# Loads of x that don't wait for the averages' matrix, and layer 1 of an outlook network with three engines in program order and its transfers a column behind their source

## The chip, the cores and the metric

One core of one Trainium2 chip runs the kernel. The metric is the device time of one execution in microseconds (us), taken as the median of several runs; a profiled execution has a span of its own, a little longer. TensorE does the matrix work (PE in the views; PEld is its weight load), VectorE (DVE) and ScalarE (ACT) the elementwise work, GpSimd (POOL) some of it, SyncE (SP) only asks for transfers. SyncE and ScalarE each ask for transfers on a queue of their own, q1 and q10 in the profile.

## What is computed

The input x is 8 images of 56 x 56 positions with 384 channels, in float32. Two layers follow one another, each x + layer(group norm of x). A layer computes values v and attention logits from every position by a projection, takes a softmax over the 9 positions of a 3 x 3 window, and weighs the values with it:

```python
def _gn(v, G=32, eps=1e-5):
    g = v.reshape(B_, H_, W_, G, C_ // G)
    m = jnp.mean(g, axis=(1, 2, 4), keepdims=True)
    s = jnp.var(g, axis=(1, 2, 4), keepdims=True)
    return ((g - m) / jnp.sqrt(s + eps)).reshape(v.shape)
...
# layer 0: 12 heads; each position has 9 x 9 weights and adds to 9 places
attn = jax.nn.softmax(a * d ** (-0.5), axis=-1)
out = jnp.einsum('bnhpq,bnqhd->bnphd', attn, v_unf).reshape(b, h, w, k2, c)
...
# layer 1: 6 heads; each position has 9 weights and gathers from 9 places
a = jax.nn.softmax(a.reshape(B, H * W, heads, k * k), axis=-1)
y = jnp.einsum('bpKhd,bphK->bphd', patches, a)
return y.reshape(B, H, W, C) @ W_proj + b_proj
...
x = x + _L0_conv_ref(_gn(x), L0_conv_Wv, L0_conv_Wa, L0_conv_Wo)
x = x + _L1_conv_ref(_gn(x), L1_conv_W_attn, L1_conv_b_attn, L1_conv_W_v, L1_conv_b_v, L1_conv_W_proj, L1_conv_b_proj)
```

## The kernel before

Two images make a pair, so there are four pairs; a column of a pair is 112 rows of one x coordinate, and there are 56 columns. Seven columns make a group (the code's `px`), eight groups a pair, 32 groups a layer.

*Start.* Pair 0 of x is loaded in 14 blocks of 4 columns (L132 in the profile, on SyncE), transposed on TensorE (L122), copied out by ScalarE into 14 "homes" all over the on-chip memory, and its statistics are taken by VectorE. Four buffers hold loaded blocks: two in `xr`, two in `vp_first`. The group averages need a matrix `gmat`, made by three matmuls from a 0/1 matrix `gsel` that GpSimd writes. `gsel` is in a pool of its own that is closed again, and the `patch` pool, opened later, lies on the same memory. `keep_block` then stores the transposed blocks to `xT` in the DRAM, in the order 2, 3, ... 13, 0, 1, since later steps read them again: `xin` has two buffers, which are the homes of blocks 0 and 1, and block 2 is loaded into the first of them. These stores are in SyncE's program order, with zero fills of the tables between them.

*Layer 0.* One step per column: three projections for logits, softmax, weights, spread into a table `ztab0` in the DRAM. Once per group, `z` (the weights, read back as bands) and `vp` (the values, read back as patches) are loaded and contracted into `yT`, which is projected and added to x. The result is stored as `x1` for layer 1.

*Layer 1.* A step of the loop is one column m of a group g. `attend` projects 128 tokens to logits and values (`bank`, from `wc_t`); VectorE adds the biases into `lgt` and `v`, and `spread` stores v to `vtab1` (ScalarE's queue). When the group's columns are through, the following go on beside the columns of the next group:

- `regroup`: logits stored to `lgtab` (ScalarE's queue), read back as `at` (SyncE's queue), both at m = 0;
- `weigh` at m = 2: maximum, subtraction (VectorE), exponential (ScalarE), sum, reciprocal (VectorE), multiplication (GpSimd);
- `move` at m = 3: three matmuls `pw`, nine small copies into `wz` (ScalarE), one store to a table `ztab1` (ScalarE's queue);
- `fetch` in the same step: `vp` loaded from `vtab1`, `z` loaded from `ztab1` (SyncE's queue), and 14 jobs put on a list: four contractions (`pc`, copied to `yT` by ScalarE), four turns, six projections (`po`, added to `x1t` by VectorE), the last three with a turn each. A turn transposes a column of the result and copies it to `ot`; after the fourth and the seventh a store to `out` follows.

The jobs fall due four columns after `fetch`; two of them run in every step, one before `attend` and one after it:

```python
jobs.run(base + step, 1)
...
jobs.run(None, 1)
fetch(g - 1, base + step + 4)
```

`load(g + 1)` of the layer's input `x1t` is asked for at m = 4, into one of four buffers; `normed` on ScalarE normalises it at m = 6 and m = 0. `z` has four buffers in the memory of layer 0's two `z` tiles.

*Order.* Only TensorE's instructions are kept in the order in which the program names them (`tc.keep_in_program_order`); a scheduler orders the other engines by its own estimates, but for the instructions of SyncE that go through the `InOrder` wrapper in layer 0. Each engine then carries out its list in order, and waits at an instruction until what it needs is there.

Of the kernel before, what the change touches and what calls it, by code (L numbers as in the profile page):

```python
# [15 lines left out]
def two_outlook_layers(  # L16
# [35 lines left out]
    P = 128  # L52
# [85 lines left out]

    shift = const.tile([R, K, R], F32, name="shift")
    nc.gpsimd.memset(shift, 0.0)  # L140
    for k in range(-1, 2):
        s = shift[:, k + 1, :]
        nc.gpsimd.affine_select(
            out=s, in_=s, compare_op=ALU.not_equal, fill=1.0,
            base=k, pattern=[[-1, R]], channel_multiplier=1,
        )
    for b in range(1, IMG):
        nc.gpsimd.memset(shift[:, 2, b * H : b * H + 1], 0.0)
        nc.gpsimd.memset(shift[:, 0, b * H - 1 : b * H], 0.0)


    PH_ALL = K * HEADS0
    inside = const.tile([R, K, PH_ALL], F32, name="inside")
    nc.gpsimd.memset(inside, 1.0)
    for b in range(IMG):
        for pi, row in ((0, b * H), (2, b * H + H - 1)):
            nc.gpsimd.affine_select(
                out=inside[:, pi, :], in_=inside[:, pi, :], compare_op=ALU.not_equal, fill=0.0,
                base=-row, pattern=[[0, PH_ALL]], channel_multiplier=1,
            )  # L160
# [3 lines left out]
    with tc.tile_pool(name="setup", bufs=1) as setup, tc.tile_pool(  # L164
        name="ps_setup", bufs=2, space=PS
    ) as ps_setup:
        gsel = setup.tile([G, C], F32, name="gsel")
        nc.gpsimd.memset(gsel, 1.0)
        nc.gpsimd.affine_select(
            out=gsel, in_=gsel, compare_op=ALU.is_ge, fill=0.0,  # L170
            base=0, pattern=[[1, C]], channel_multiplier=-GC,
        )
        nc.gpsimd.affine_select(
            out=gsel, in_=gsel, compare_op=ALU.is_ge, fill=0.0,
            base=GC - 1, pattern=[[-1, C]], channel_multiplier=GC,
        )
        for i in range(NCH):
            pg = ps_setup.tile([P, C], F32, tag="pg", name=f"pg_{i}")
            matmul(pg, gsel[:, i * P : (i + 1) * P], gsel, start=True, stop=True)
            nc.vector.tensor_scalar_mul(gmat[:, i, :], pg, 1.0 / GC)  # L180

    NZERO = (EP0 - E0) * ROW0
    zeros = const.tile([R, NZERO], F32, name="zeros")
    nc.gpsimd.memset(zeros, 0.0)
# [51 lines left out]
    nc.gpsimd.memset(eps_t, EPS)  # L236
# [119 lines left out]
    patch = ctx.enter_context(tc.tile_pool(name="patch", bufs=2))  # L356
# [11 lines left out]
    def projected(name):  # L368
        return patch.tile([P, NCH, PX, IMG, H], F32, tag="yT", name=f"yT_{name}", bufs=1)

    def rows_to_patches(vp, table, px, r0, py, npy, sx):
        first = (px * (R + GAP) + GAP - MARGIN + r0) * sx * C
        nc.sync.dma_start(
            vp,
            bass.AP(
                table.tensor, table.offset + first, [[C, vp.shape[0]], [py * sx * C, npy], [1, C]]
            ),
        )
# [13 lines left out]
    def layer0(late, pools):  # L392
# [49 lines left out]
        def blocks_in(flat, n, at=0):  # L442
# [19 lines left out]
            *blocks_in(projected("first").rearrange("p i m b y -> p (i m b y)"), 1),  # L462
# [6 lines left out]

        def first_load(blk):  # L470
            xr = more[:R, blk // 2 % 2] if blk % 2 else xr_tile(0, blk)
            stats_load(0, blk, sync, xr)

        sync = InOrder(nc.sync)
        NXR = 4
# [26 lines left out]
        for i in range(NCH):  # L502
            for pi in range(K):
                natural = wn[:, i, pi * NP0 : (pi + 1) * NP0].rearrange("c (j q h) -> c q j h", j=K, q=K2)
                nc.gpsimd.tensor_tensor(
                    wa_t[:, i, pi * NL : (pi + 1) * NL].rearrange("c (q j h) -> c q j h", q=K2 - 1, j=K),
                    natural[:, : K2 - 1],
                    natural[:, K2 - 1 :].to_broadcast([P, K2 - 1, K, HEADS0]),
                    ALU.subtract,
                )  # L510
# [113 lines left out]
        def fetch_v(pair, px):  # L624

            vps[:] = [patch_tiles(f"0_{pair}_{px}", b) for b in range(IMG)]
            for b in range(IMG):
                rows_to_patches(vps[b], vtab0, px, b * H, PY0, NPY0, SX0)
# [80 lines left out]
        def upkeep(step):  # L709

            pair, c = divmod(step, W)
            if pair == 0:

                for n in (2 * step, 2 * step + 1):
                    if n < NBLK:
                        keep_block(0, (n + 2) % NBLK)
                if c == 3:
                    sync.dma_start(wo_t, wo0.rearrange("(i p) n -> p i n", p=P))
                if c == 8:
                    for z in zs:  # L720
                        nc.gpsimd.memset(z, 0.0)
# [56 lines left out]
    def layer1(pools, base, last_of_layer0, late_w):  # L778
        io = pools.enter_context(tc.tile_pool(name="io1", bufs=2))
# [4 lines left out]

        def load(g):
            pair, px = divmod(g, NPX)

            if g % 4 == 3:
                t = late_w.tile([P, NCH, T], F32, tag="xres", name=f"x1t_{g}")
            else:  # L790
                t = io.tile([P, NCH, T], F32, tag="x1t", name=f"x1t_{g}", bufs=3)
            nc.sync.dma_start(t, x1s[pair][px])
            x1ts[g] = t.rearrange("p i (m r) -> p i m r", m=PX)

        def normed(g, m0, m1):
# [4 lines left out]
            for lo, hi in ((first + m0, min(cut, first + m1)), (cut, first + m1)):  # L800
# [3 lines left out]
                for i in range(NCH):  # L804
                    for b in range(IMG):
                        rows = slice(b * H, (b + 1) * H)
                        nc.scalar.activation(  # L807
                            to[:, i, :, rows], x1ts[g][:, i, lo - first : hi - first, rows],
                            AF.Identity,
                            bias=bias[:, i, b : b + 1], scale=scale[:, i, b : b + 1],  # L810
                        )
# [5 lines left out]
        nc.sync.dma_start(wc_t[:, :, :NA1], wa1.rearrange("(i p) n -> p i n", p=P))  # L817
        nc.sync.dma_start(wc_t[:, :, NA1:], wv1.rearrange("(i p) n -> p i n", p=P))
# [8 lines left out]

        NZ = 4
        half_z = NPY1 * PY1 * ROW1
        zs1 = [  # L830
            zs[n // 2].rearrange("p n e -> p (n e)")[: SX1 * SY1, n % 2 * half_z : (n % 2 + 1) * half_z]
            .rearrange("p (n e) -> p n e", n=NPY1)
            for n in range(NZ)
        ]

        def attend(g, m):

            col = g * PX + m
            if col % SB == 0:
                return  # L840
# [5 lines left out]
            nc.vector.tensor_add(staged[-1][1][:, len(staged[-1][0])], pa[:, :NA1], ba_t)  # L846
            staged[-1][0].append(col // SB * NT + tile_no)
            v = work.tile([P, C], F32, tag="v", name=f"v_1_{col}", bufs=5)
            nc.vector.tensor_add(v, pa[:, NA1:], bv_t)  # L849
            for lo, n_col, row, n in parts_of(tile_no):  # L850
                c = col - col % SB + n_col
                spread(nc.scalar, vtab1, SX1, c % W, 1, row, v[lo : lo + n])
# [6 lines left out]
        def regroup(g):  # L859
# [3 lines left out]
            nc.scalar.dma_start(  # L863
# [5 lines left out]
            )  # L869
            lgs[g] = work.tile([R, PX, K2, HEADS1], F32, tag="at", name=f"at_1_{g}")  # L870
            nc.sync.dma_start(
# [7 lines left out]

        def weigh(g):  # L880

            at = lgs[g]
            heads_last = [R, PX, K2, HEADS1]
            mx = work.tile([R, PX, HEADS1], F32, tag="mx", name=f"mx1_{g}")
            nc.vector.tensor_reduce(mx, at.rearrange("r x k h -> r x h k"), AX.X, ALU.max)
            nc.vector.tensor_tensor(at, at, mx.unsqueeze(2).to_broadcast(heads_last), ALU.subtract)
            nc.scalar.activation(at, at, AF.Exp)
            den = work.tile([R, PX, HEADS1], F32, tag="den", name=f"den1_{g}")
            nc.vector.tensor_reduce(den, at.rearrange("r x k h -> r x h k"), AX.X, ALU.add)
            nc.vector.reciprocal(den, den)  # L890
            nc.gpsimd.tensor_tensor(at, at, den.unsqueeze(2).to_broadcast(heads_last), ALU.mult)  # L891

        def move(g):
# [14 lines left out]
            for kj in range(K):  # L908
                dst = wz[:, kj * K * ROW1 : kj * K * ROW1 + PX * step].rearrange("r (m e) -> r m e", e=step)
                dst = dst[:, :, : K * ROW1].rearrange("r m (e h o) -> r e m h o", e=K, h=HEADS1)  # L910
                for e in range(K):
                    nc.scalar.copy(dst[:, e, :, :, 0], pw[:, e, :, kj, :])
            table = ztab1[g % NTAB]
            nc.scalar.dma_start(
# [7 lines left out]
        def fetch(g, due):  # L922
# [5 lines left out]
            for b in range(IMG):  # L928
                rows_to_patches(vps[b], vtab1, px, b * H + MARGIN - 1, PY1, NPY1, SX1)
            for b in range(IMG):  # L930
                z, vp = zs1[(g * IMG + b) % NZ], vps[b]
                bands(
                    nc.sync, z, ztab1[g % NTAB], LINE1, SLOT1, ROW1, MARGIN - 1, GROUPS1,
                    b, PY1, NPY1,
                )

                def contract(t, b=b, z=z, vp=vp):
# [12 lines left out]
                    nc.scalar.copy(  # L950
# [9 lines left out]
            def project_out(half, j):  # L960
# [5 lines left out]
                nc.vector.scalar_tensor_tensor(  # L966
# [3 lines left out]
            def turn(m):  # L970
# [8 lines left out]
                nc.scalar.copy(fetch.ot[:, m - lo, :], pt)  # L979
                if m == hi - 1:  # L980
                    nc.sync.dma_start(
# [17 lines left out]
        for step in range(NG * PX + 4):  # L999
            g, m = divmod(step, PX)  # L1000
            jobs.run(base + step, 1)
            if step == 0:
                last_of_layer0(base + step + 5)
            if step == 4:
                for wz in wzs:
                    nc.gpsimd.memset(wz, 0.0)
            if g < NG:
                attend(g, m)
            if g and m == 0:
                regroup(g - 1)  # L1010
                stage(g)
            if m == 4 and g + 1 < NG:
                load(g + 1)
# [4 lines left out]
            jobs.run(base + step, 1)  # L1018

            if g and m == 2:  # L1020
                weigh(g - 1)
            if g and m == 3:
                move(g - 1)
                while not clear_bands.done:
                    jobs.run(None, 1)
                fetch(g - 1, base + step + 4)
# [47 lines left out]
```

## Time and profile before

| what | value |
|---|---|
| median of 3 runs | 3564.13 us (3562.12 to 3565.1) |
| span of the profiled execution | 3582.0 us, mean granted clock of TensorE 0.982 |
| layer 0's columns begin / end | about 64.6 us / 2313 us |
| first and last store lgtab<-lgt | 2375.2 us / 3525.9 us |
| DMA | 839.34 MB, 234 GB/s on average |

Busy time is in us with its share of the span. In the slices each digit is a fortieth of the span, in tenths. A group's line gives engine, operation, tiles as out<-in, count, busy time, and the idle time of the engine before it with what ended it. What the transfers of layer 1 take from issue to landing (median, us):

```profile
vp<-vtab SPq DMA_DIRECT2D x64, 945.0 KB, 10.7
...
x1t<-x SPq DMA_DIRECT2D x32, 1176.0 KB, 10.9
...
z<-ztab SPq DMA_DIRECT2D x128, 258.4 KB, 5.5
```

And what SyncE itself waited for in layer 1, from 2420 us on (us in total, times, longest):

```profile
SPq L871 <- DMA lgtab<-lgt: 370.0, 30, 18.2
SPq L320 <- DMA ztab<-wz: 297.6, 31, 13.8
SPq L373 <- DMA vtab<-v: 144.0, 25, 9.8
SPq L981 <- ACT ot L979: 63.7, 22, 13.0
```

L871 is the read of `at`, L320 the read of `z`, L373 that of `vp`, L981 the store of `out`.

### The profile page before, as it was taken

What the parts mean: (1) busy time and instruction counts of PE and PEld (TensorE: products, weight loads), DVE (VectorE), ACT (ScalarE), POOL (GpSimd) and SP (SyncE); (2) the same over time, 40 slices, a digit from 0 to 9 for tenths busy, and PEclk for the clock granted to TensorE, in tenths of its full rate; (3) what the DMA queues carried; (4) which work ended last, traced back from release to release, by engine and by line L of the source; (5) the groups of instructions that cost most, each with busy time, mean ns of one, the idle gap of its engine ahead of it and who ended that gap; (6) DMA issues with size and microseconds to landing.
All of it is one profiled execution on the core that took longest, in us unless ns stands there. A gap on an engine that the chain in (4) does not pass through costs nothing. (4 is left out here: it accounts for less than half of the span.)

```text
span 3582.0 us, 72091 instructions
## 1 busy us (share of the span) xinstructions
PE 3460.1 (97%) x29014; PEld 2370.5 (66%) x29014; DVE 1918.4 (54%) x4648; ACT 1165.9 (33%) x2727; POOL 986.7 (28%) x1409
## 2 busy tenths in 40 slices
PE   7799999999999999999999999989999999999998
PEld 5577767777777777677767777655565665656555
DVE  5666666667766766677666666533222222222222
ACT  3233323332333233333223322232333433334332
POOL 3443444434443444334434444410000000000000
PEclk8899999999999999999999999999999999999999
DMA  7999988688877777887667676687778787778876
GB/s 238 274 299 278 270 274 272 211 252 265 282 237 238 247 248 248 258 275 249 213 194 246 214 223 228 223 266 192 208 198 225 192 215 207 201 210 212 217 215 160
DMA packets 691453, 839.34 MB, mean 234 GB/s; under 512 B 302191, under 2 KB 595375, under 8 KB 687023
## 3 DMA queue, kind: packets, MB, share of 16 engines
q1 hardware_dynamic: 329614, 576.00, 50.9%
q10 hardware_dynamic: 361504, 258.73, 26.9%
q8 instruction: 228, 3.74, 0.4%
q14 instruction: 107, 0.87, 0.1%
HBM read 512.95 MB, written 321.66 MB: 233 GB/s over the span
## 5 line engine op out<-in xcount | busy, mean ns | idle before, releaser
L119 PE MATMUL bank<-wa_t,xn 128*112 128x288 f32 x4032 | 1088.3, 409 | 19.7 <-ACT xn L529 16.5
L119 PEld LDWEIGHTS bank<-wa_t,xn 128*112 128x112 f32 x4032 | 693.9, 177 | 272.8 <-issue 33.4
L119 PE MATMUL po<-yT,wo_t 128*128 128x448 f32 (+1 forms) x2304 | 818.8, 495 | 5.3 <-DVE x1t L679 4.8
L568 POOL TENSOR_TENSOR at<-at,den 112x972 f32<-112x972 f32 x224 | 504.8, 2254 | 1157.9 <-DVE den L567 1105.1
L119 PEld LDWEIGHTS po<-yT,wo_t 128*128 128x128 f32 x2304 | 432.8, 191 | 293.7 <-issue 189.4
L119 PE MATMUL pc<-z,vp 121*32 121x49 f32 (+1 forms) x17664 | 494.4, 256 | 44.2 <-DMA z<-ztab 19.6
L119 PEld LDWEIGHTS pc<-z,vp 121*32 121x32 f32 (+1 forms) x17664 | 448.1, 132 | 121.1 <-issue 94.4
L119 PE MATMUL bank<-wc_t,xn 128*128 128x438 f32 x1176 | 496.7, 560 | 4.4 <-DMA wc_t<-in_wv 3.2
L544 DVE TENSOR_REDUCE mx<-bank 112x36 f32<-112x324 f32 x672 | 327.4, 487 | 323.1 <-PE bank L119 316.0
L119 PE MATMUL bank<-wv_t,xn 128*128 128x384 f32 x1176 | 419.2, 493 | 0.0
L891 POOL TENSOR_TENSOR at<-at,den 112x378 f32<-112x378 f32 x32 | 30.2, 944 | 1132.0 <-DVE den L890 853.9
L119 PEld LDWEIGHTS bank<-wc_t,xn 128*128 128x128 f32 x1176 | 220.3, 197 | 183.0 <-issue 172.2
L545 DVE TENSOR_TENSOR at<-bank,mx 112x324 f32<-112x324 f32 x672 | 328.5, 489 | 21.0 <-DVE den L567 0.3
L549 ACT ACTIVATE at<-at 112x972 f32<-112x972 f32 x224 | 227.0, 1014 | 343.6 <-DVE at L545 319.6
L807 ACT ACTIVATE xn<-x1t,bias,scale 128x168 f32<-128x168 f32 (+4 forms) x498 | 213.7, 503 | 324.7 <-DMA x1t<-x 236.9
L119 PEld LDWEIGHTS bank<-wv_t,xn 128*128 128x128 f32 x1176 | 219.9, 191 | 140.0 <-issue 19.3
L966 DVE SCALAR_TENSOR_TENSOR x1t<-po,bo_t,x1t 128x448 f32<-128x448 f32 (+1 forms) x192 | 120.1, 625 | 322.9 <-PE po L119 322.9
L846 DVE TENSOR_TENSOR lgt<-bank,ba_t 128x54 f32<-128x54 f32 x196 | 41.3, 211 | 440.0 <-PE bank L119 439.8
L591 POOL TENSOR_TENSOR pre<-at,at 112x108 f32<-112x108 f32 (+1 forms) x440 | 239.0, 543 | 125.3 <-DVE wt L614 110.7
L613 ACT COPY wt<-pw 112x120 f32<-112x120 f32 x224 | 58.0, 259 | 659.3 <-PE pw L119 607.5
L561 DVE TENSOR_TENSOR d<-at 112x432 f32<-112x432 f32 x224 | 141.3, 631 | 199.7 <-ACT at L549 199.7
L658 ACT COPY yT<-pc 128x294 f32<-128x294 f32 x256 | 103.4, 408 | 372.2 <-PE pc L119 327.0
(95 smaller groups left out, 2818.5 us busy)
## 6 DMA issues: line engine op xcount, KB each, us to landing
z<-ztab SPq DMA_DIRECT2D x64, 2352.0 KB, 15.6
vp<-vtab SPq DMA_DIRECT2D x64, 1536.0 KB, 7.4
ztab<-wt ACTq DMA_DIRECT2D x336, 183.8 KB, 6.3
vp<-vtab SPq DMA_DIRECT2D x64, 945.0 KB, 10.7
xres<-xT SPq DMA_DIRECT2D x32, 1176.0 KB, 11.2
x1t<-x SPq DMA_DIRECT2D x32, 1176.0 KB, 10.9
xin<-xT ACTq DMA_DIRECT2D x54, 672.0 KB, 4.9
z<-ztab SPq DMA_DIRECT2D x128, 258.4 KB, 5.5
```

The source lines that it names most:

```text
L119: tc.keep_in_program_order(nc.tensor.matmul(*args, **kwargs))
L544: nc.vector.tensor_reduce(mx[:, pi, :], pl.rearrange("r q a -> r a q"), AX.X, ALU.max)
L545: nc.vector.tensor_tensor(at[:, pi], pl, mx[:, pi, :].unsqueeze(1).to_broadcast([R, K2, PH]), ALU.subtract)
L549: nc.scalar.activation(at, at, AF.Exp, scale=SCALE0)
L561: nc.vector.tensor_add(d4, at[:, :, 0:4], at[:, :, 4:8])
L568: nc.gpsimd.tensor_tensor(at, at, den.unsqueeze(2).to_broadcast([R, K, K2, PH]), ALU.mult)
L591: nc.gpsimd.tensor_tensor(dst, terms[0], terms[1], ALU.add)
L613: nc.scalar.copy(mid[:, 0 : E0 : E0 - 1, :], pw[:, 0 : E0 : E0 - 1, :])
L658: nc.scalar.copy(yT[:, :, :, b, rows_of], pc.rearrange("p i n y m -> p i m (n y)"))
L807: nc.scalar.activation(to[:, i, :, rows], x1ts[g][:, i, lo - first : hi - first, rows], AF.Identity, bias=bias[:, i, b : b + 1], scale=sca ...
L846: nc.vector.tensor_add(staged[-1][1][:, len(staged[-1][0])], pa[:, :NA1], ba_t)
L966: nc.vector.scalar_tensor_tensor(res, po[:, :n], bo_t[:, j : j + 1], res, ALU.add, ALU.add)
```

## The change

At the start, `gsel` is put into the memory of `yT`, and GpSimd makes it first, in program order. The loads of x into `vp_first` have nothing to wait for any more. The blocks 0 and 1 are kept second, after 2 and 3. In layer 1, VectorE, ScalarE and SyncE are put in program order. Each transfer is asked for about a column after the work that makes its source, so that an engine that waits in its list waits little. `regroup` becomes `keep_logits` (m = 0) and `read_logits` (m = 1); `weigh` is split into `weigh` (m = 3, to the exponential) and `share` (m = 4); `move` is at m = 5 and `fetch` at m = 0 of the group after, with the jobs due three columns later. Within `fetch`, `z` is read before `vp`. `x1t` is loaded at m = 1 and has five buffers; the fifth is a half of a `z` tile, so `z` has three buffers left. The stores of `v` come behind the second job of their step, and the stores of `out` go to ScalarE's queue. The last group runs through these steps faster (`last`).

```diff
+    gpsimd = InOrder(nc.gpsimd)
+    patch = ctx.enter_context(tc.tile_pool(name="patch", bufs=2))
+    yT_first = projected("first")
+    yT_flat = yT_first.rearrange("p i m b y -> p (i m b y)")
...
-        gsel = setup.tile([G, C], F32, name="gsel")
-        nc.gpsimd.memset(gsel, 1.0)
+        gsel = yT_flat[:G, :C]
+        gpsimd.memset(gsel, 1.0)
...
-            xr = more[:R, blk // 2 % 2] if blk % 2 else xr_tile(0, blk)
+            xr = more[:R, blk % 2] if blk % NXR > 1 else xr_tile(0, blk)
...
-                        keep_block(0, (n + 2) % NBLK)
+                        keep_block(0, n ^ 2 if n < 4 else n)
...
     def layer1(pools, base, last_of_layer0, late_w):
+        vector, scalar, sync = (InOrder(e) for e in (nc.vector, nc.scalar, nc.sync))
...
-            if g % 4 == 3:
+            if g % 5 == 3:
                 t = late_w.tile([P, NCH, T], F32, tag="xres", name=f"x1t_{g}")
+            elif g % 5 == 4:
+                t = halves[3][:, : NCH * T].rearrange("p (i t) -> p i t", i=NCH)
...
             for b in range(IMG):
-                rows_to_patches(vps[b], vtab1, px, b * H + MARGIN - 1, PY1, NPY1, SX1)
+                bands(
+                    sync, zs1[(g * IMG + b) % NZ], ztab1[g % NTAB], LINE1, SLOT1, ROW1, MARGIN - 1,
+                    GROUPS1, b, PY1, NPY1,
+                )
+            for b in range(IMG):
+                rows_to_patches(sync, vps[b], vtab1, px, b * H + MARGIN - 1, PY1, NPY1, SX1)
...
-                    nc.sync.dma_start(
+                    scalar.dma_start(
                         of[pair * R : (pair + 1) * R, px * PX + lo : px * PX + hi, :],
...
-        for step in range(NG * PX + 4):
+        for step in range((NG + 1) * PX):
             g, m = divmod(step, PX)
+            done, last = g - 1, g == NG
+            read, first, second, moved = (0, 2, 3, 4) if last else (1, 3, 4, 5)
             jobs.run(base + step, 1)
...
+            if g and m == first:
+                weigh(done)
+            if g and m == second:
+                share(done)
+            if g and m == moved:
+                move(done)
+            store = lambda: None
             if g < NG:
-                attend(g, m)
+                store = attend(g, m)
+            jobs.run(base + step, 1)
             if g and m == 0:
-                regroup(g - 1)
+                keep_logits(done)
                 stage(g)
-            if m == 4 and g + 1 < NG:
-                load(g + 1)
+            store()
             if m == 6 and g + 1 < NG:
                 normed(g + 1, 0, 3)
             if m == 0 and 0 < g < NG:
                 normed(g, 3, PX)
-            jobs.run(base + step, 1)
-            if g and m == 2:
-                weigh(g - 1)
-            if g and m == 3:
-                move(g - 1)
+            if m == 1 and g + 1 < NG:
+                load(g + 1)
+            if g > 1 and m == 0:
                 while not clear_bands.done:
                     jobs.run(None, 1)
-                fetch(g - 1, base + step + 4)
+                fetch(done - 1, base + step + 3)
+            if g and m == read:
+                read_logits(done)
+            if last and m == 5:
+                fetch(done, base + step + 1)
```

## The prediction

> **What bounds the kernel now.** I read the page's shares and slices first, then TensorE's busy time by stage, then what TensorE waits for, then the chain that ended last.
>
> ```profile
> PE 3460.1 (97%) x29014; PEld 2370.5 (66%) x29014; DVE 1918.4 (54%) x4648; ACT 1165.9 (33%) x2727; POOL 986.7 (28%) x1409
> ...
> PE   7799999999999999999999999989999999999998
> ```
>
> TensorE is the bound. The change removes no matmul, so it can only win back time in which TensorE waits. The windows (columns: stretch, its length, PE busy and instructions, granted clock, DMA share, GB/s) say where that is:
>
> ```profile
> 0.00:20.00 20.00, 9.62 (x33) 1.00 0.65 188
> 20.00:50.00 30.00, 23.27 (x122) 0.84 1.02 287
> 50.00:100.00 50.00, 43.07 (x187) 0.89 0.66 231
> 100.00:200.00 100.00, 81.05 (x418) 0.90 0.94 292
> ...
> 500.00:1000.00 500.00, 499.60 (x4479) 1.00 0.80 252
> ...
> 2800.00:3000.00 200.00, 190.26 (x1356) 0.94 0.78 210
> 3000.00:3200.00 200.00, 191.02 (x1426) 0.97 0.78 204
> ```
>
> Three stages: the start (up to 200 us) has 43 us of idle TensorE; layer 0 after it has almost none; layer 1 (2313 us on) loses some 5% again, and there the granted clock dips too. One wait at the start and the waits of layer 1 (window 2420 to the end; us in total, times, longest):
>
> ```profile
> 120.16 0.55 PE L122 MATMUL pt<-ident,xr 112*128 112x112 f32 x4
> 134.98 5.35 PE L119 MATMUL bank<-wa_t,xn 128*112 128x288 f32 x12 [14.27 <-ACT xn L529]
> ```
> ```profile
> ACT xn L807 <- DMA x1t<-x: 236.9, 22, 12.7
> ...
> PE pc L119 <- DMA z<-ztab: 16.2, 10, 3.0
> PE pw L119 <- POOL at L891: 13.4, 11, 2.7
> ```
>
> The listed waits of TensorE in layer 1 are short: 48 us in all (the two above, 11.3 without a named cause, 5.6 on the copies out of pc, 1.6 on ot). Behind them stands the chain of one group:
>
> ```profile
> 2800.45 12.59 DMA ztab<-wz
> 2813.43 4.44 DMA z<-ztab
> 2818.01 2.12 PE pc L119 x48
> ```
> ```profile
> 2397.55 6.31 DMA ztab<-wz
> ```
>
> The weight table takes 12.6 us to land when SyncE's queue carries vp and x1t beside it. In the first group it is 6.3 us, and there, by the trace's packets, the first 2.5 stood beside the end of an x1t load; then its 1,008 packets passed in about 2 us. Then z is read, and the contraction waits for it.
>
> The pace: the 32 stores lgtab<-lgt are issued from 2375.2 to 3525.9 us, so a group takes 37.1 us. Its matmuls at full clock, by their start-to-start times: wc_t 2.2 us x 49 tiles in 8 groups = 13.5; pc 2 x (1.55 + 1.20) = 5.5; po 3 x 2.26 + 3 x 1.70 = 11.9; seven transposes 3.0; pw 0.7. Sum 34.6 us. So 31 groups hold 78 us of loss, waits and slow clock together.
>
> **What the Trainium skill says.** "TensorE: Matmul & The Clock Gate", Part 1 (The HAM clock gate): after an idle window TensorE's clock is halved until it has been busy for a while. The trace agrees: behind the 14.27 us wait twelve matmuls took 5.35 us against 3.08 elsewhere, and after the 2.05 us wait at 2818 the next six took 3.57 against 2.47. So a wait of 2 us costs up to 4. "DMA: Bandwidth & Descriptors", Queues, rings and completion order: SyncE and ScalarE own one queue each on the same 16 engines, each consumed in order, the engines alternating between the two. The trace agrees: an x1t load issued at 2840.75 had its first packet at 2845.5, behind the vp and out packets asked for before it. "PSUM — Partial Sum Buffer", Engine vs sequencer instructions: VectorE's and ScalarE's queues are strictly first in, first out, so an early wait blocks all behind it. The trace agrees: transposes into pt ended at 2809.7 and were copied at 2813.0, behind a normalisation that waited for x1t until 2811.75.
>
> **The change part by part.**
> *Start.* Before, the second to fourth load of x go out at 9.43 us, when the matmuls on gsel have read a buffer that vp_first lies on; after, gsel lies in yT, and four loads go out from 0.8 us. From 20 to 50 us the DMA share is 1.02: the 11.0 MB issued from 9.43 us end by some 51, which is about 268 GB/s. All 11.7 MB from 1.5 us at that rate end at 45: -6.5 us. The gsel steps move to the head of GpSimd's list (from 5.1 to about 3 us, the sum of the durations before it), which keeps TensorE ready for it.
> *Blocks 0 and 1 kept early.* The xin load of block 2 needs the buffer of block 0, whose store goes last (issued 110.8 to 125.5). That is the 14.27 us wait and 2.3 us of slow clock. With the order 2, 3, 0, 1 the store goes out before 60 us, and block 2 is due at about 102: the wait vanishes. DMA is at 0.94 there and gets less time for the same stores, and the two 4 us memsets of z now stand between GpSimd's multiplications; I give back 3 us. Start in all: -20 us (10 to 27).
> *x1t loads* three columns earlier, with a fifth buffer: ends the 236.9 us for which ScalarE stood at the normalisation. TensorE waited 1.2 us for that; by itself nothing.
> *Logits, weights, contraction.* weigh moves from m=2 to 3, share 4, move from 3 to 5, the contraction from four columns behind the move to five. Columns m=0..2 hold two po jobs and take 6.5 us, m=3..6 about 4.2. The logits and ztab get slack, and pw's 13.4 us and z's 16.2 us of waits lose their old cause.
> *Program order on SyncE.* The list is now, per group: 4 z, 2 vp, x1t, at. The z reads wait for ztab, and vp, x1t and at stand behind them, on one queue. The at read, which took 2.5 us to land with the queue to itself, now lands behind 4 MB. From it follow weigh, pw, ztab, and the next z: a loop that goes round once per group. Its length, from landing of at to landing of the next:
> - at to issue of ztab: mx, subtract, exp, den, reciprocal, the GpSimd multiply, pw and nine copies took 6.6 us in the last group (3533.1 to 3539.7). In program order exp holds up ScalarE, and about 2 us of the copies and DMA issues it held stand before the nine: 8.3 us.
> - ztab to the first z packet: SyncE's queue is empty then. 1.2 us to ztab's first packet, 2.0 for its packets, 1.3 until SyncE is released, 1.1 to z's first packet: 5.6. Bounds: this, and the 8.5 us that the last group's ztab took beside vp and an out store, 9.6 in all. I take the lower, as nothing of SyncE's is under way.
> - By the packets of the trace a group costs the 16 engines 5.3 us for z, 8.0 for vp, 2.9 for x1t, 0.8 for at: 17.0. ScalarE's queue puts about 4.1 between (lgtab 0.8, vtab of three columns 2.2, the rest of an out store). 21.1 at the 1.05 that the share reaches when both queues run: 20.1 us.
> - to VectorE's start: 0.6.
> Sum 34.6 us, the same as TensorE's own. So the loop and TensorE set the pace together, and a late landing in either is a wait of 1 or 2 us at the contraction or pw of m=5, since exp holds the copies that free pc. With 1 us of such waits and slow clock per group I take 35.6: 31 x (35.6 - 37.1) = -46 us.
> *Ends.* First logits behind an x1t load: +5 us. At the end z stands before vp and the contraction comes later, but six more po jobs and the whole of group 30 cover the last chain; before, 2.7 us of wait stood there. In all +4 us.
> *out stores* on ScalarE's queue instead of SyncE's (3.8 us of engines per group): hidden, counted above.
> Sum: -20 - 46 + 4 = -62: 3502 us; I say 3500.
>
> **Rivals.**
> *TensorE's pace alone*, as the change intends: at lands within some 23 us of m=0 and no wait is left. For it: z, vp and weigh have slack in columns. Against: the loop's sum leaves none. With 0.3 us of small waits per group: 31 x (34.9 - 37.1) = -68, start -20, ends +2: 3478 us.
> *The loop sets the pace clearly.* More of ScalarE's stores between, or a ztab of 6.5: 36.8 us. 31 x 0.3 = -9, start -20, ends +4: 3539 us. For it: DMA has no idle stretch between ztab and at, so all that is late adds.
> *The loop is much longer, and the time gets worse.* ztab at 8.5 as in the last group, since out stores and vtab stand before it in ScalarE's queue: 34.6 + 4.0 = 38.6 us. 31 x 1.5 = +47, ends +4, start -20: 3595 us. For it: the chain of before shows what sharing does to ztab (12.6). Against: SyncE's queue is empty while ztab is written.
> *The start gives nothing*, because DMA is at 0.94 to 1.02 there and the wait turns up later: 3522 us with the rest as forecast. Against it: the window 50 to 100 us has a share of 0.66.
>
> **How the numbers follow.** Both set the pace (35.2 to 36.2 us, 3488 to 3522; the start that gives nothing counted in): 0.45. TensorE's pace: 0.18. The loop clearly (to 37.5, 3560): 0.22. Much longer: 0.15. The first two are faster, of the third nine in ten, of the last none: faster by over 0.2% (below 3557) 0.82, within 0.2% (to 3571) 0.05, slower 0.13. Range 3465 to 3575: below lies a TensorE that never waits together with a start that gives its most, above the last case but its edge.
>
> **What would show it.** Right: at<-lgtab taking over 10 us to land instead of 2.5; VectorE's mx waiting for it in many groups; the lgtab stores 35 to 36 us apart; DMA still near 0.8 with idle stretches while at is worked on; the 14.27 us gone. Wrong: lgtab stores under 35 us apart and mx never waiting (then TensorE's pace), or 37 and more (then the longer loops); the 14 us turning up in another ScalarE wait before 200 us; SyncE issuing vp or x1t ahead of z.

## The result, and the profile after

The changed kernel takes 3614.69 us (3612.19 to 3625.53) against 3564.61 us: 1.014 times the time of before, 95% interval 1.012 to 1.0161. It is slower by 50 us; 62 us less had been forecast. The profiled execution of before lies 17 us above its median, so the two traces show only 3614.5 - 3582.0 = 32.5 us of the 50.

Shares and slices of the changed kernel's page:

```profile
PE 3459.2 (96%) x29014; PEld 2362.1 (65%) x29014; DVE 1918.4 (53%) x4648; ACT 1180.6 (33%) x2727; POOL 985.7 (27%) x1409
...
PE   7899999999999999999999999889999999999998
```

TensorE is busy for the same time as before (3460.1), with the same instructions: in these two traces all of the loss is idle TensorE, 155 us instead of 122. The windows, in the same stretches as before (stretch, length, PE busy and instructions, clock, DMA share, GB/s):

```profile
0.00:20.00 20.00, 11.54 (x55) 0.97 0.88 264
20.00:50.00 30.00, 17.85 (x122) 0.78 1.03 313
50.00:100.00 50.00, 44.82 (x175) 0.83 0.66 219
100.00:200.00 100.00, 85.73 (x532) 0.97 0.97 305
500.00:1000.00 500.00, 499.77 (x4476) 1.00 0.82 257
2800.00:3000.00 200.00, 191.14 (x1465) 0.98 0.77 207
3000.00:3200.00 200.00, 186.49 (x1445) 0.98 0.75 203
```

The start does slightly better, and layer 0 is as it was. The place of work tells more than busy time: the last four matmuls of pw in layer 0 come at 2313.3 us instead of 2324.5, so the start brought 11 us between these two traces (in the traces of the experiments with the same start they come at 2312.6 to 2323.2 us). The first store of lgtab comes only 4.5 us earlier (2370.7), the last one 18.3 us later (3544.2), and from there to the end it is 70.3 us instead of 56.1. A group takes 37.86 us instead of 37.12. TensorE's work in the tail, from the last store on, grew by 9.1 us, because a group is now finished later; its idle time there grew by 5. So the opening of layer 1 gives back 7 of the 11 us, and the groups lose most: the stretch between the first and the last store is 22.8 us longer, and TensorE is idle in it for 79.5 us instead of 51.3. TensorE's waits in layer 1 (waits of the changed kernel from 2420 to 3540 us; total, times, longest):

```profile
PE pc L119 <- ACT yT L132: 40.4, 24, 3.8
PE bank L119 <- ACT xn L132: 27.7, 22, 2.2
```

These two had been 5.6 and 0; z and pw, for which TensorE waited 29.6 us before, are gone from the list. ScalarE had become the engine that TensorE waits for. The timeline of ScalarE ahead of one such wait (start, length, instruction; ACTq is the issue of a transfer; in brackets the idle time before):

```profile
2695.46 0.52 ACT L132 ACTIVATE at<-at 112x378 f32<-112x378 f32 x1 [3.70 <-DVE at L132]
2695.88 0.46 ACT L132 COPY ot<-bank 112x384 f32<-112x384 f32 x1
2696.37 0.33 ACTq L132 DMA_DIRECT2D out<-ot  x1
2696.80 2.22 ACTq L132 DMA_DIRECT2D vtab<-v  x2
2699.06 0.44 ACT L132 COPY yT<-pc 128x336 f32<-128x336 f32 x1 [2.72 <-DVE v L132]
```

The contraction that TensorE runs next needs the last copy, at 2699.06. Ahead of it in ScalarE's list stand exp, late because at had landed late (VectorE's mx, the maximum that opens the softmax, waited for at in 28 groups, 103 us in all), and then three issues of transfers. The second vtab issue alone lasts 1.80 us: over 48 such triples of out, vtab, vtab the last one takes 1.53 us (median), where the last of lgtab, vtab, vtab took 0.47 before. The same triple stands at m = 6 ahead of the normalisation. The chain of waits through this stretch (window 2690 to 2735) ties all of it together:

```profile
2686.17 7.73 DMA at<-lgtab
2693.90 0.02 issue
2693.92 0.85 DVE mx L132
...
2697.22 1.80 ACTq L132
2699.02 0.04 issue
2699.06 0.45 ACT yT L132
2699.51 0.04 issue
2699.55 1.61 PE pc L119 x48
2701.16 1.03 PE pw L119 x6
...
2711.54 1.60 ACTq L132
2713.14 0.05 issue
2713.19 0.65 ACT xn L132 x2
...
2716.86 13.24 DMA lgtab<-lgt
...
2730.16 2.77 DMA at<-lgtab
2732.93 0.02 issue
2732.96 0.84 DVE mx L132
```

It starts and ends at the same point of two groups: a loop. Over the window 2420 to 3540 us, the same chain by line begins:

```profile
by line: PE bank L119 24.2%; DMA at<-lgtab 16.2%; DMA lgtab<-lgt 12.0%; PE po L119 10.9%; PE pc L119 10.5%; ACTq L132 8.0%; ACT xn L132 3.0%; PE pw L119 2.8%; issue 1.9%; PE pt L122 1.6%; DVE den L132 1.6%; PE bank L122 1.5%; DVE mx L132 1.
```

In the kernel before (window 2420 to 3500) it had been:

```profile
by line: PE bank L119 23.8%; DMA ztab<-wz 17.7%; PE po L119 13.4%; PE pc L119 9.9%; DMA vtab<-v 6.5%; DMA z<-ztab 6.0%; DMA lgtab<-lgt 3.1%; issue 2.0%; DMA at<-lgtab 1.9%; ACTq L308 1.7%; DMA x1t<-x 1.7%; PE pt L122 1.5%; DMA vp<-vtab 1.3%
```

There ztab held 17.7%, lgtab and at together 5.0%; now these two hold 28.2% and ScalarE's issues 8.0%, and ztab and z have left the chain. Two suspects, then: at lands late behind what SyncE asks for ahead of it, and ScalarE is held at its issues behind an out store.

### The profile page after: what moved, and what is told of

Its sections match the earlier page's. It is cut to its first block, busy times and chain, and to the rows that moved or that the text cites. A ratio compares the mean times of both kernels' runs of the same rounds, so it can differ in the third digit from the quotient of the medians.

```text
span 3614.5 us, 72141 instructions
## 1 busy us (share of the span) xinstructions
PE 3459.2 (96%) x29014; PEld 2362.1 (65%) x29014; DVE 1918.4 (53%) x4648; ACT 1180.6 (33%) x2727; POOL 985.7 (27%) x1409
## 5 line engine op out<-in xcount | busy, mean ns | idle before, releaser
L132 DVE SCALAR_TENSOR_TENSOR x1t<-po,bo_t,x1t 128x448 f32<-128x448 f32 (+1 forms) x156 | 97.6, 626 | 249.0 <-PE po L119 249.0
L132 ACT ACTIVATE xn<-x1t,bias,scale 128x168 f32<-128x168 f32 (+4 forms) x402 | 168.0, 500 | 123.3 <-issue 83.1
```

The lines of the kernel that those rows point to most:

```text
L132: return lambda *args, **kwargs: tc.keep_in_program_order(op(*args, **kwargs))
```

## The experiments

The kernel before took 3577 to 3590 us on the chips of the experiments, so ratios to it are what is compared; the changed kernel stands at 1.014. Theory 1 is ScalarE's list with its held issue, theory 2 is SyncE's loop.

**Out stores back on SyncE's list.**

```diff
-                    scalar.dma_start(
+                    sync.dma_start(
                         of[pair * R : (pair + 1) * R, px * PX + lo : px * PX + hi, :],
```

> The changed kernel, with its out stores on SyncE's list again and no longer on ScalarE's. Theory 1 (ScalarE's list: in the changed kernel's trace the second vtab issue behind an out store takes 1.5 us instead of 0.45, and copies of pc and the normalisation stand behind the three issues): the waits pc<-ACT yT (45 us) and bank<-ACT xn (33 us) shrink to under 25 us together, lgtab stores 36.3 to 36.8 us apart instead of 37.85, 3560 to 3580 us. Theory 2 (SyncE's loop: the at read behind z, vp and x1t is late): both waits stay above 60 us together, the stores also queue before z, 3610 to 3630 us.

Measured: 3680.8 us, ratio 1.0294 (1.0275 to 1.0314). Neither time was met; the two waits stay above 60 us together, as theory 2 has it. TensorE's waits from 2420 to 3600 us:

```profile
PE pc L119 <- ACT yT L132: 88.1, 29, 4.9
PE pc L119 <- DMA vp<-vtab: 16.9, 9, 5.4
PE bank L119 <- ACT xn L132: 1.7, 4, 0.7
```

The wait for xn at m = 6 vanishes, as theory 1 has it; but mx waits 225 us for at instead of 103, and a group takes 39.9 us. In program order the second out store now stands before the next z reads: from the issue of ztab to that of z it is 6.4 us instead of 4.2 (means of 28 groups), and SyncE's packets between z and at take 19.6 us of the engines instead of 17.2. So what is put into SyncE's list between ztab and at is paid for.

**The read of at ahead of z.**

```diff
+            if g and m == 0:
+                read_logits(done)
             if g > 1 and m == 0:
...
-            if g and m == read:
-                read_logits(done)
```

> The changed kernel, with the read of at put ahead of the z reads in SyncE's list, so that nothing of a group's 4 MB stands before it. Theory 2 (SyncE's loop): VectorE's mx no longer waits for at and exp no longer holds ScalarE's list, pc<-ACT yT falls from 45 to under 15 us, lgtab stores under 37 us apart, 3570 to 3585 us. Theory 1 (the issues on ScalarE): exp goes away as a cause, but the third issue still takes 1.5 us ahead of the copies; pc<-ACT yT falls by some 15 to 25 us, bank<-ACT xn stays at 30 us or above, 3590 to 3605 us.

Measured: 3726.75 us, 1.0432 (1.0409 to 1.0456). A miss for both, and my edit is to blame. To stand ahead of z, at is read a column earlier. VectorE no longer waits for at, but z waits behind it for the logits to be stored. z is asked for 14.6 us after the issue of ztab instead of 4.2, and vp lands too late for the contraction at m = 3 (same view):

```profile
PE pc L119 <- DMA vp<-vtab: 96.5, 28, 14.9
PE bank L119 <- ACT xn L132: 24.2, 22, 1.3
PE pc L119 <- ACT yT L132: 8.1, 6, 1.9
```

pc's wait for ScalarE fell from 40 to 8 us, as theory 2 has it, and the wait for xn stayed near its 28, as theory 1 has it. A list in program order has no place where a wait costs nothing: what is put first has to be ready first.

**The start alone.** Everything up to layer 1 as changed, layer 1 as before.

> The start of the changed kernel (loads of x, order of the kept blocks, GpSimd's order) with layer 1 of the kernel before. If the start's gain holds (the two traces stand 11.9 us apart at the last pw of layer 0): 3550 to 3556 us, and all of the loss lies in layer 1. If the start gives nothing: 3562 to 3567 us. My forecast had 20 us here: 3545 us.

Measured: ratio 0.9973 (0.9958 to 0.9989), 3566.4 against 3577.3 us. The start is worth 10 us (4 to 15), near the 11 between the traces of before and after, about half of what I gave it; all of the loss lies in layer 1.

**The out store behind the vtab stores of its column**, still on ScalarE. The store is put on a list and issued right after `store()`:

```diff
-                    scalar.dma_start(
+                    late_out.append(lambda ot=fetch.ot: scalar.dma_start(
...
             store()
+            while late_out:
+                late_out.pop(0)()
```

> The changed kernel, with each out store on ScalarE issued after the two vtab stores of its column instead of before them. Theory 1a (an issue that follows an out store is held): nothing of ScalarE's issues stands right behind the store, the vtab issues take 0.45 us again, and ScalarE comes to the copies and normalisations 1.1 us earlier: both waits together fall from 78 to 30 to 50 us, 3585 to 3600 us. Theory 1b (the third of three issues in a row is held, whatever it is): the out store's issue takes 1.5 us instead, the time stays at 3610 to 3618 us. Theory 2 (SyncE's loop): 3610 to 3618 us as well, with vtab issues at 0.45 us.

Measured: 3577.42 us, 0.9999 (0.9987 to 1.0012): 1.4% less than the changed kernel from moving two issues per group by two places, more than theory 1a asked for. ScalarE's timeline at the two places:

```profile
2686.93 0.79 ACTq L132 DMA_DIRECT2D vtab<-v  x2
2687.81 0.38 ACTq L132 DMA_DIRECT2D out<-ot  x1
2688.23 0.64 ACT L132 COPY yT<-pc 128x336 f32<-128x336 f32 x2 [1.00 <-DVE den L132]
...
2698.05 0.79 ACTq L132 DMA_DIRECT2D vtab<-v  x2
2698.94 0.40 ACTq L132 DMA_DIRECT2D out<-ot  x1
2699.38 3.96 ACT L132 ACTIVATE xn<-x1t,bias,scale 128x112 f32<-128x112 f32 x11 [1.24 <-issue]
```

Two vtab issues take 0.79 us here, not 2.2, and the out store's 0.4; the median of the third issue is 0.39. So it isn't the third of three issues that is held, but the second one that soon follows an out store. Such issues have become few, and are still held: of 19 that came second behind an out store and within 2 us of it, 14 took over 1 us, of the 39 later ones only one; in the changed kernel it was 46 of 50 within 2 us (window 2420 to 3540). From 2420 to 3540 us the waits for yT and xn are 35.8 and 8.4 us. A group takes 36.6 us. ScalarE stands less at its issues, so from mx to the issue of ztab it is 7.8 us instead of 9.35 (means of 28 groups), but the chain by line still has 17.1% each for lgtab and at.

**The read of at ahead of the x1t load.** Two requests of one column change places:

```diff
-            if m == 1 and g + 1 < NG:
-                load(g + 1)
...
             if g and m == read:
                 read_logits(done)
+            if m == 1 and g + 1 < NG:
+                load(g + 1)
```

> The changed kernel, with the read of at put ahead of the x1t load in the same column of SyncE's list; nothing else moves. If the loop (at, exp, ScalarE's copies, pc, pw, ztab, z, vp, x1t, at) sets the pace of layer 1: the x1t packets (2.9 us of the engines) leave it, a group falls from 37.96 us to 35.8 to 36.6, and the ratio to the kernel before from 1.014 to 1.000 to 1.006. If the hold behind the out store sets it alone and the late at costs nothing: a group stays at 37.5 or above, the ratio at 1.011 or above.

Measured: 3572.04 us, 0.9984 (0.9972 to 0.9995), a little better than forecast. mx starts 14.9 us behind the store of lgtab instead of 17.2 (medians), and a group takes 36.4 us. ScalarE's third issue still takes 1.44 us behind out (median of 50). The chain by line from 2420 to 3500 us:

```profile
by line: PE bank L119 38.7%; PE po L119 26.7%; PE pc L119 14.3%; ACTq L132 5.1%; PE pt L122 3.1%; PE pw L119 2.5%; PE bank L122 2.4%; ACT xn L132 1.4%; DMA at<-lgtab 1.3%; ACT ot L132 1.0%; issue 1.0%; ACT yT L132 0.7%; DMA lgtab<-lgt 0.7%; 
```

lgtab and at have gone from 28% to 2%: waiting for at is no longer on the longest path, TensorE's own work is.

**Both edits.**

> Both: the out store issued behind the vtab stores, and the read of at ahead of the x1t load. If the loop still sets the pace when one of the two is taken away (36.66 us a group with the out store moved), the second takes another 1 us: 35.2 to 35.8 us a group, ratio 0.986 to 0.992, pc<-ACT yT under 12 us. If what was left had another cause (TensorE's own pace with the slow clock): 36.3 us or above, ratio 0.997 to 1.001.

Measured: 3541.49 us, 0.9887 (0.9868 to 0.9907); once more beside a later run, 3543.73 us, 0.9871 (0.9855 to 0.9887), for which the expectation was:

> The version with both edits once more, on the chip of this call, for the comparison with the normalisation moved. Expected as before: ratio 0.987 to 0.991.

A group takes 35.25 us, and TensorE works 198.9 us of the window 2800 to 3000. Alone the two edits take 1.4 and 1.6 points off the ratio of 1.014, together 2.5: nearly the sum. What is missing from it is likely TensorE's own pace.

**Program order engine by engine**: the wrapper taken off ScalarE, off SyncE, or off all three, everything else as changed.

```diff
-        vector, scalar, sync = (InOrder(e) for e in (nc.vector, nc.scalar, nc.sync))
+        vector, scalar, sync = InOrder(nc.vector), nc.scalar, InOrder(nc.sync)
```

> The changed kernel with the scheduler's order on ScalarE instead of the program's; VectorE and SyncE as changed. The normalisations then stand in pieces between the copies, and the out stores mostly no longer ahead of two vtab stores. If program order on ScalarE is what costs: bank<-ACT xn and pc<-ACT yT fall from 78 to under 40 us together, ratio 0.998 to 1.005. If it is SyncE's list that costs: at is as late as before, both waits stay above 60 us, ratio 1.010 or above.

> The changed kernel with the scheduler's order on SyncE alone; ScalarE and VectorE stay in the program's. SyncE then asks for z, x1t and at, and for vp behind at. If it is SyncE's written order that makes at late and so sets the pace: VectorE's mx starts 3 us or more earlier behind the lgtab store than the 17.2 us of the changed kernel, ratio 0.993 to 1.003. If it needs ScalarE's order to go as well, because the 1.5 us behind the out store stays: 1.006 to 1.012.

> The changed kernel with the scheduler's order on VectorE, ScalarE and SyncE: the columns, buffers and queues of the change stay. The scheduler puts the at read ahead of vp, and vp behind it. If program order as such costs the time: ratio 0.990 to 1.000. If the new place of vp makes the contraction wait for vp, as it did with the read put first (108 us of pc<-DMA vp): ratio 1.010 to 1.040.

Measured: ScalarE free 1.0078 (1.0054 to 1.0102), SyncE free 0.9958 (0.994 to 0.9976), all free 0.9927 (0.9903 to 0.995). With ScalarE free the wait for xn is 1.6 us, but mx starts 20.1 us behind the store of lgtab and pc still waits 46.6 us for ScalarE: between the two forecasts. With SyncE free, mx starts at 14.9, 2.3 us earlier than in the changed kernel instead of the 3 asked for. With all free, the changed kernel's columns, buffers and queues are 26 us better than the kernel before, 10 of which are the start's. So the new columns, buffers and queues together are worth something. Most of the loss goes with the order in which the program names SyncE's requests (1.8 points of the ratio), less with ScalarE's (0.6). The two don't simply add up: all free is 0.3 points under SyncE free, and their intervals overlap. VectorE's order alone wasn't tried.

**The normalisation ahead of the vtab stores at m = 6**, on top of both edits.

```diff
+            if m == 6 and g + 1 < NG:
+                normed(g + 1, 0, 3)
             store()
...
-            if m == 6 and g + 1 < NG:
-                normed(g + 1, 0, 3)
```

> The kernel with the out store behind the vtab stores and the read of at ahead of x1t, and with the normalisation of the next three columns ahead of the vtab stores of m=6 on ScalarE. If ScalarE's list still costs TensorE its waits for xn (8.6 us in all from 2440 us on): those go, 3540 less 5 to 10 us, 0.1 to 0.3% under the version without this edit, beside it on the same chip. If TensorE's own pace is what is left: no difference beyond 0.1%.

Measured: 3528.23 us, 0.9836 (0.9816 to 0.9856), 15.5 us under the version without it on the same chip, more than forecast. The windows:

```profile
2800.00:3000.00 200.00, 199.11 (x1577) 1.00 0.83 224
3000.00:3200.00 200.00, 197.32 (x1543) 1.00 0.85 222
```

TensorE no longer waits for xn in layer 1's steady part, a group takes 34.8 us, and this version beats the kernel before by 1.6% and the changed one by 3.0%. It gains more than the 8.9 us of listed waits that it removes. The traces show where: between the first and the last store of lgtab TensorE is idle for 6.3 us less, and the projection's matmuls, as many as before, are busy for 434.6 us instead of 444.9. Their weight loads had waited for xn 70 times, 47.6 us in all, mostly in pieces too short for the list of TensorE's waits; now it is 3.8 us. Less slow clock is not the reason: 13.7 us of that stretch ran at half clock, against 10.2 without the edit.

## Why the prediction was wrong

*The bound* held: TensorE's busy time is the same to 1 us in the two traces, and only waits changed.

*Start, -20 us:* right in kind. The 14.27 us wait is gone. But the start gave 10 us timed. The loads of x out early were put at 6.5 us and gave about 4: layer 0's first column begins at 60.7 us instead of 64.6 (59.9 to 62.0 in the other traces with this start), and TensorE waits 14.3 us for loads of x in place of 11.0. Behind that, in place of the 14.27 us, TensorE waits for GpSimd's pre (7.5 us up to 200 us instead of 1.9), for ScalarE's v (4.8 instead of 3.2) and xn (3.6), with DMA at 0.97 from 100 to 200 us. I gave back 3 us where some 10 were due.

*x1t loads, nothing by themselves:* ScalarE's 237 us at the normalisation did end. What became of ScalarE in their stead wasn't asked.

*Program order on SyncE* is the step that failed. That at would land late behind z, vp and x1t was right, but the sum of 34.6 us, and the pace of 35.6 taken from it, were too short. The terms of the loop, as means of 28 groups from the changed kernel's trace:

| term | forecast | measured |
|---|---|---|
| mx (at has landed) to issue of ztab | 8.3 | 9.35 |
| issue of ztab to first z packet | 5.6 | 5.3 (4.19 to z's issue, and my 1.1) |
| first z packet to mx | 20.1 + 0.6 | 23.2 |
| loop | 34.6 | 37.87, the pace of the groups |

The sum was 3.3 us short, 2.5 of them in the last term and 1.05 in the first. SyncE's packets in the last term took 17.2 us of the engines, the 17.0 forecast. ScalarE's took 5.7 instead of 4.1, and the engines were busy at 0.98, not at the 1.05 that I divided by: 22.9 us of packets in 23.2 us. In the kernel before they had been busy at 0.65 in that leg. The requests don't come in one go: SyncE asks for vp only 4.9 us behind z, and at is issued when lgtab has landed, 9 us behind its store. (In the trace eight semaphores, used in turn by the transfers of both queues, tell of landings; 20 of SyncE's requests waited for a z to land, nearly all of them vp reads, which have no need of z.) The first term holds what the next step left out.

These legs run from one event of a group to the same event of the next, so they add up to the pace whatever bounds it; what speaks for this loop are the full engines and the two experiments that lengthened it (out stores back on SyncE's list) and shortened it (at ahead of x1t). The chain of waits comes back to at by another way: exp, ScalarE's issues, the copy of yT, pc, TensorE's columns, the normalisation, the store of lgtab. I had no term for that way. The store of lgtab took 8.9 us to land (median) instead of 3.6. Both ways end in at, and each of the two edits that helped shortens both, so the runs don't tell which of them sets the pace.

*"out stores on ScalarE's queue ...: hidden, counted above"* is the other term that failed, put at nothing. They were counted as 3.8 us of the engines; the time of ScalarE's own list wasn't. An out store there makes the issue two places on last 1.53 us, twice a group, ahead of the copies and the normalisation that TensorE needs next. Moving the store two places brought 1.4% back. Moving at ahead of x1t brought 1.6%, so either term alone made the difference between level and slower; with both repaired the ratio is 0.989, and with the normalisation moved as well 0.984, near the 0.983 that I had forecast. The section "Engine vs sequencer instructions" of the Trainium skill's "PSUM — Partial Sum Buffer" was cited for an early wait that blocks all behind it. I applied that to SyncE's list and to exp, not to ScalarE's issues; the 2.22 us of issues ahead of yT's copy are the same rule at work.

*Ends, +4 us:* TensorE's idle time in the tail grew by 5. The opening of layer 1 was missed: some 7 us of the start's gain went there, among it 4.8 us at the first contraction, which waits for vp, now asked for behind z (before, 3.4 us for z).

*Rivals:* "much longer", 38.6 us a group and 3595 us, came nearest (37.87) and was given 0.15. Its reason was wrong: it put the 4 us on ztab, and ztab was on time. The sign named there (stores 37 us and more apart) is what showed up. As for the sign of being right, from the issue of at to mx it took 8.4 us (median of 28), not over 10.

One reading in the forecast was rough: of the x1t load issued at 2840.75 us, 9 of its 128 packets passed before 2845.5, the first at 2841.93; the rest did stand behind vp and out.

What stays open: why an issue behind an out store is held. In the stretch shown above, the 112 packets of 6144 bytes of the out store pass from 2697.2 us on, and the held issue ends at 2699.02, when 95 of them have started. How much of the store has passed doesn't decide it: behind 25 stores of 672 KB the held issue took 1.55 us (median) and ended with 80 to 96 packets started, behind 24 of 504 KB it took 1.26 us, and 18 of those ended with 3 to 6 started.

## What to carry to other kernels

When requests are put into program order, draw the loop that the order closes over one round, through every list it passes and not only the one that is reordered, and add up each leg at the share that the transfers reach in that stage; where its sum is within a few us of the bound, the bound isn't safe. An issue of a transfer is an instruction of the engine that asks for it: what stands behind it on that engine, and who waits for that, has to be priced like a computation. A read that everything waits for goes ahead of a load that is needed columns later: here one exchange of two requests was worth 1.6%.

## What the runs showed of the hardware

A transfer issue on ScalarE took 0.4 us (median), but 1.53 us (median of 48, up to 1.88) when it was the second one behind an out store of 672 or 504 KB, issued 0.85 us after it. With the out store behind the two vtab stores, its own issue took 0.39 us, and second issues that came over 2 us after it were held once in 39. In the kernel before, which had no out stores on ScalarE, 20 of the 425 issues from 2420 to 3540 us took over 1 us as well, so an out store isn't the only cause.

Short waits were enough for the slow clock. In layer 1 of all thirteen traces (from 2420 us to the last store of lgtab), a stretch of 3.4 to 10.2 us at half clock began during the wait or within 3 us of its end for 49 of TensorE's 50 waits of 3 us and more, 47 of 57 from 2 to 3 us, 30 of 57 from 1.5 to 2 us, and 7 of 89 from 1 to 1.5 us. The one exception among the longest is a wait of 3.06 us in the changed kernel: the group from 2560.9 us reads a clock of 1.00, while the one from 2483.8, with waits of 2.1 and 1.0 us, reads 0.917. Fewer waits pay twice: between the first and the last store of lgtab, TensorE ran at half clock for 61.4 us in the changed kernel (68.3 before) and for 10.2 with both edits.
